# Attention's value products and score products of a gated cross-attention kernel, issued as 64x64 tiles of TensorE

## The chip, the cores and the metric

The kernel runs on one core of one Trainium2 chip. The metric is the device time of one execution in microseconds. The kernel before was timed three times: 958.02, 959.36 and 960.18 us, median 959.36 us. A profile is one further execution, recorded by the hardware profiler.

## The reference

Eight batches `b`, 1024 tokens each with `D` = 1024 features, attend to 64 memory rows of 512 features. All is fp32.

```python
memory_proj = einsum('bme,de->bmd', memory, W_mem)
scores = einsum('bnd,bmd->bnm', hidden, memory_proj) / sqrt(D)
attn = softmax(scores, axis=-1)
memory_context = einsum('bnm,bmd->bnd', attn, memory_proj)
gate_input = concatenate([hidden, memory_context], axis=-1)
gate = sigmoid(einsum('bnf,df->bnd', gate_input, W_gate) + b_gate)
fused = hidden + gate * memory_context
out = fused * rsqrt(mean(fused**2, axis=-1) + 1e-6) * norm_w
```

## The kernel before, in words

The tokens are cut into 16 groups `q` of 512 tokens, two groups to a batch. A group is four blocks of 128 tokens. In a setup stage the kernel projects the memory (`mp`, 64 rows by 1024) and multiplies the projected memory by the second half of the gate's weight. The two results stand one above the other in one tile `mg` of 128 partitions: rows 0 to 63 hold the projected memory, rows 64 to 127 its product with the gate weight and the bias. So `attn` times the upper half is `memory_context`, and `attn` times the lower half is that context's share of the gate's input.

The remaining large product is `x` times the first half of the gate's weight, 512 x 1024 by 1024 x 1024 for a group. It is computed with two nested levels of a Strassen-like scheme: seven outer products in the order `ORDER = (1, 6, 7, 5, 4, 2, 3)`, each of seven inner products of 128x128 by 128x256 (function `outer_product`). Each outer product accumulates in two PSUM banks, `af` and `ed`, for which there are two sets of names that alternate (`af0`, `ed0`, `af1`, `ed1`); two further inner products go to banks `b` (tile `kB`) and `c` (tile `kC`). The last two PSUM banks are a rotating pair with the tag `ctx`. VectorE (DVE) adds the inner sums `u2`, `u3`, `u4` and, with `fin_af` and `fin_ed`, adds a bank into the output rows (`gate` in the profile, `O` in the code). GpSimd (POOL) makes inner operand sums (`inner_s`) and part of the output sums (`pre`).

**Visits.** A visit (function `visit`) is the part of attention's value product that belongs to one row pair and one half of the 1024 columns: for each of the two blocks `r` it multiplies the transposed attention by `mg[0:64]` into a bank of its own (`pcs`, `pc` in the profile) and by `mg[64:128]` into `af` or `ed`, where it is added to the outer product's sum. Visits come in pairs, inside outer products 4 and 3, after the inner product `kC`: the visit of the outer product before last (5 or 2, whose banks `faf` and `fed` were kept), with its `pc` in banks `b` and `c`, and then the visit of the running outer product, with its `pc` in the `ctx` pair. There are 32 such pairs, two per group. ScalarE (ACT) then applies the sigmoid to a `gate` half, and DVE multiplies it by `pc` (function `gated`).

**Scores.** For each group, `scores` multiplies `mp` by the transposed tokens `A` over eight slices `k` of the features, one matmul for each of two row pairs `r`, all into bank `b`. ScalarE copies the bank to SBUF (`sT`); `transpose_scores` turns it by TensorE some slots later, and the softmax follows. The scores of group `q + 1` are issued inside outer product 3 of group `q`, directly after its two visits. Since bank `b` holds a `pc` there, ScalarE first copies that `pc` to SBUF (`pe`, L905), and the later multiplication reads the copy. The scores of group 0 stand between outer products 1 and 6 of group 0.

**Order.** The order within each engine is the order of the code: every instruction is pinned in program order. `plan` assigns side work to slots (`at`, 49 slots a group, one per inner product) or to named places inside an outer product (`mid` with a key; `beside.pop` runs it). In outer product 3 the named places come in this order: both visits, place `(q, 3, 0)`, the sums of the visit that was kept (`fin_af`, `fin_ed` of outer product 2, with their sigmoids), place `(q, 3)`, then the step to the next slot. Place `(q, 3, 0)` holds one DVE transpose of the next group's tokens; place `(q, 3)` holds the next group's scores, two large DVE sums (`outer_s` 1 and 2) and a normalisation.

Of the kernel before, what the change touches and what calls it, by code (L numbers as in the profile page):

```python
# [10 lines left out]
ALU = mybir.AluOpType  # L11
# [4 lines left out]
P = 128  # L16
# [4 lines left out]
def tile_gated_cross_attention_rmsnorm(  # L21
# [376 lines left out]

    def scores(q):

        pst = bank("b", [P, 2 * P], f"psT{q}")
        mpb = mps[q // QPB]
        for k in range(KD):
            for r in range(2):
                mm(
                    pst[r * M : (r + 1) * M, :],
                    mpb[:, k, :],
                    A[q, r, k // KH][:, k % KH, :],
                    k == 0,
                    k == KD - 1,  # L410
                )
        sTs[q] = t4k(small, [P, 2, P], "e", f"sT{q}")
        pin(nc.scalar.copy(sTs[q].rearrange("p t c -> p (t c)"), pst))

    def transpose_scores(q):
        sc = ps_ctx.tile([P, 4, M], F32, tag="ctx", name=f"sc{q}")
# [199 lines left out]
    def plan(q):  # L616
        t0 = SLOTS * q
        nxt = q + 1 < NQ
        for i, o in enumerate(ORDER):
            for part, t in ((0, 1), (1, 2)):  # L620
                if i + 1 < len(ORDER):
                    at(t0 + 7 * i + t, inner_s, q, ORDER[i + 1], part)
                elif nxt:
                    at(t0 + 7 * i + t, inner_s, q + 1, ORDER[0], part)
        if q == 0:
            at(t0 + 7, scores, q)
        at(t0 + (3 if q else 7), outer_s, q, 3)
        at(t0 + (11 if q else 22), outer_s, q, 4)
        at(t0 + 9, transpose_scores, q)
        at(t0 + 10, softmax_a, q)  # L630
        at(t0 + 13, softmax_b, q)
        at(t0 + 18, transpose_attn, q)
        at(t0 + 22, attn_difference, q)
        if not nxt:
            at(t0 + 5, load_last)
            return
        at(t0 + 2, load_xq, q + 1)
        for i, t, half in (
            (20, 0, 0), (21, 1, 0), (23, 2, 0), (25, 3, 0), (37, 2, 1), (38, 3, 1), (42, 0, 1)
        ):  # L640
            at(t0 + i, transpose_x, q + 1, t, half)
        mid((q, 3, 0), transpose_x, q + 1, 1, 1)
        mid((q, 3), scores, q + 1)
        mid((q, 3), outer_s, q + 1, 1)
        mid((q, 3), outer_s, q + 1, 2)
        if (q + 1) % QPB == 0:
            at(t0 + 10, load_mp, (q + 1) // QPB)
            at(t0 + 49, load_mg, (q + 1) // QPB)
        if q == 0:
            at(t0 + 8, add_bias, mgs[0][M:P, :])  # L650
            at(t0 + 20, add_bias, mgd[1, M:, :])
# [149 lines left out]
    EXT = {5: (1, 1, 2), 4: (1, 0, 2), 2: (0, 0, 0), 3: (0, 1, 4)}  # L801
    SECOND = {4: 5, 3: 2}
    NEG = {4: 6, 3: 7}
    sets = 0
    held = {}

    def visit(q, o, pcs, af, ed):

        row, h, g = EXT[o]
        at_, mg = attnTs[q], mgs[q // QPB]  # L810
        second = o in SECOND
        for r, k in ((0, af), (1, ed)):
            for n in range(2):
                cols = slice(h * H + n * C, h * H + (n + 1) * C)
                mm(
                    pcs[r][:, n * C : (n + 1) * C],
                    at_[0:M, 2 * row + r, :],
                    mg[0:M, cols],
                    n == 0,
                    True,  # L820
                )
                left = NEG[o] if second and r == 0 and n == 1 else g + r
                mm(k[:, n], at_[M:P, left, :], mg[M:P, cols], second and r == 1 and n == 0, True)

    def pre(q, o, u3, u4):

# [39 lines left out]
    def outer_product(q, o):  # L866

        nonlocal slot, sets
        l11, l12, l21, l22 = quarters(left(q, o))
        s1, s2, s3, s4 = (L2[q, o][:, i, :, :] for i in range(4))  # L870
        nxt = q + 1 < NQ
        af = bank(f"af{sets}", [P, 2, C], f"af{q}_{o}")
        ed = bank(f"ed{sets}", [P, 2, C], f"ed{q}_{o}")
        sets ^= 1
        second = o in SECOND

        def product(out, lhsT, s, start):
            nonlocal slot
            for k in range(2):
                mm(out, lhsT[:, k, :], w_op(o, s)[:, k, :], start and k == 0, k == 1)  # L880
            slot += 1

        ut = t4k(rot, [P, 4, C], "u", f"u{q}_{o}")
        p1, u2, u3, u4 = (ut[:, i, :] for i in range(4))
        step()
        product(af[:, 0], l11, R11, True)
        pin(nc.scalar.copy(p1, af[:, 0]))  # L887
        step()
        kb = bank("b", [P, C], f"kB{q}_{o}")
        product(kb, s2, T2, True)  # L890
        tt(nc.vector, u2, p1, kb, ALU.add)
        step()
        kc = bank("c", [P, C], f"kC{q}_{o}")
        product(kc, s3, R12, True)
        tt(nc.vector, u3, u2, kc, ALU.add)
        pre(q, o, u3, None)
        if second:
            f = SECOND[o]
            faf, fed, fu3, fu4 = held.pop((q, f))
            frow, fh, _ = EXT[f]  # L900
            fp = [bank(t, [P, H], f"pc{q}_{f}_{r}") for r, t in enumerate("bc")]
            visit(q, f, fp, faf, fed)
            if o == 3 and nxt:
                pe = t4k(small, [P, H], "pe", f"pe{q}")
                pin(nc.scalar.copy(pe, fp[0]))  # L905
                fp[0] = pe
            pcs = [ps_ctx.tile([P, H], F32, tag="ctx", name=f"pc{q}_{o}_{r}") for r in range(2)]
            visit(q, o, pcs, af, ed)
        for fn in beside.pop((q, o, 0), ()):
            fn()  # L910
        if second:
            one = slice(0, 1)
            fin_af(q, f, faf, fu4, one)
            gate(q, 2 * frow, fh, fp[0], 0)
            fin_ed(q, f, fed, fu3, one)
            gate(q, 2 * frow + 1, fh, fp[1], 1)
            rest = slice(1, 2)
            fin_af(q, f, faf, fu4, rest)
            fin_ed(q, f, fed, fu3, rest)
        for fn in beside.pop((q, o), ()):  # L920
            fn()
        step()
        product(ed[:, 0], l22, T4, not second)
        step()
        product(ed[:, 1], s1, T1, False)
        tt(nc.vector, u4, u2, ed[:, 1], ALU.add)
        pre(q, o, None, u4)
        first = o in SECOND.values()
        if first:
            held[q, o] = af, ed, u3, u4  # L930
        else:
            fin_ed(q, o, ed, u3)
        if second:
            row, h, _ = EXT[o]
            gate(q, 2 * row + 1, h, pcs[1], 2 if o == 3 and not nxt else 1)
        step()
        product(af[:, 1], s4, R22, False)
        step()
        product(af[:, 0], l12, R21, False)
        if not first:  # L940
            fin_af(q, o, af, u4)
        if second:
            if o == 4 and not nxt:
                at(slot + 1, gate, q, 2 * row, h, pcs[0], 1)
            else:
                gate(q, 2 * row, h, pcs[0], 1)
        if second and not nxt:
            c, d = 2 * row, 2 * row + 1
            if o == 3:
                sqrt_table()  # L950
            when = (3, 4, 4, None, 10, 11) if o == 4 else (0, 2, 2, 2, 3, 3)
            if o == 4:
                for h_ in range(2):
                    mid((q, 3, 0), last_weigh, c, h_)
            at(slot + when[0], last_root, d)
            at(slot + when[1], last_root, c)
            for w_, (t, h_) in zip(when[2:], ((d, 0), (d, 1), (c, 0), (c, 1))):
                if w_ is None:
                    mid((q, 3, 0), last_norm, t, h_)
                else:  # L960
                    at(slot + w_, last_norm, t, h_)
        elif second:

            c, d = 2 * row, 2 * row + 1
            for t in (d, c):
                at(slot + 5, residual, q, t)
            if row == 0:
                when = (17, 18, -1, None, 33, -2) if q + 2 < NQ else (17, 18, 20, 22, 24, 25)
            else:
                when = (17, 18, 22, 24, 29, 31)  # L970
            at(slot + when[0], square, q, c)
            at(slot + when[1], square, q, d)
            for w_, (t, h_) in zip(when[2:], ((c, 0), (c, 1), (d, 0), (d, 1))):
                if w_ is None:
                    mid((q + 1, 4), norm, q, t, h_)
                elif w_ < 0:
                    mid((q + 1, 4, 0) if w_ == -1 else (q + 1, 3), norm, q, t, h_)
                else:
                    at(slot + w_, norm, q, t, h_)
        del L2[q, o]  # L980
# [34 lines left out]
```

## Time and profile before

| | |
|---|---|
| median of three runs | 959.36 us |
| the profiled execution | 957.75 us |
| its span, first to last instruction | 956.0 us |
| granted TensorE clock | 0.997 |
| TensorE matmuls busy | 943.6 us, 99% of the span |
| VectorE busy | 811.4 us, 85% |
| GpSimd busy | 717.3 us, 75% |
| ScalarE busy | 371.0 us, 39% |

The page counts one fp32 matmul as two matmul records and two weight loads (PE and PEld), since it is run in two passes; 4984 records of each are 2492 matmuls. A form such as 64\*128 is the part of TensorE's array that an instruction uses, rows by columns: 128\*128 is the whole array, 64\*128 a row tile, 128\*64 a column tile. Matmuls overlap, so the distance between two starts, not the length of one record, is what a matmul costs in a stream.

### The profile page before, as it was taken

Reading aid. Unit: us, or ns where it says so; the run is one execution under the profiler, and the core shown is the slowest. Engines: PE = TensorE matmul, PEld = TensorE weight load, DVE = VectorE, ACT = ScalarE, POOL = GpSimd, SP = SyncE. Lnnn points to the kernel's source line nnn. Section 1 sums busy time; section 2 is a strip of 40 time slices with the busy share of each in tenths; the row PEclk is TensorE's granted clock in tenths of the full one; section 3 lists DMA queues with packets and bytes.
Section 4 is the critical chain, followed back from the end, with each engine's and each line's share of the span. In section 5 each row is a group of like instructions: output and inputs, shape, how many; then the busy total and the mean of one; then the engine's idle time right before and its main releaser. Section 6 shows DMA issues by size and latency. Waiting matters only on the chain.

```text
span 956.0 us, 14301 instructions
## 1 busy us (share of the span) xinstructions
PE 943.6 (99%) x4984; PEld 778.2 (81%) x4984; DVE 811.4 (85%) x1242; ACT 371.0 (39%) x797; POOL 717.3 (75%) x780
## 2 busy tenths in 40 slices
PE   9999999999999999999999999999999999999995
PEld 8546888888888888888888888888888888888884
DVE  6988888888888888888888888978888888878887
ACT  3001235262533535262433526252443526252456
POOL 4998877678676777787676867777686767877683
PEclk9999999999999999999999999999999999999998
DMA  9866674472919264481919265391918365390712
GB/s 381 270 152 152 113 126 107 123 164 52 202 45 196 91 138 117 110 177 43 211 45 186 84 147 125 93 194 32 222 46 173 92 143 133 85 203 26 217 67 89
DMA packets 70919, 128.33 MB, mean 134 GB/s; under 512 B 12352, under 2 KB 49216, under 8 KB 70592
## 3 DMA queue, kind: packets, MB, share of 16 engines
q1 hardware_dynamic: 61664, 93.86, 37.1%
q0 software_dynamic: 9184, 33.56, 19.2%
q8 instruction: 40, 0.66, 0.3%
q14 instruction: 31, 0.25, 0.1%
HBM read 87.56 MB, written 41.68 MB: 135 GB/s over the span
## 4 chain that ended last, share of the span: by engine, by line
PE 97%; DVE 1%; DMA 1%; ACT 0%; issue 0%; POOL 0%; SPq 0%; DVEq 0%
PE af L92 30%; PE ed L92 21%; PE pc L92 12%; PE kC L92 10%; PE kB L92 10%; PE psT L92 6%; PE pg L92 5%; PE pm L92 2%; DMA wm<-in_w_mem_t 1%; PE pa L451 0%; PE sc L420 0%; DVE gate L702 0%; DVE gate L776 0%; DVE u L95 0%; DVE gate L95 0%
## 5 line engine op out<-in xcount | busy, mean ns | idle before, releaser
L95 POOL TENSOR_TENSOR gate<-gate,u 128x512 f32<-128x512 f32 (+1 forms) x224 | 243.2, 1098 | 184.4 <-DVE u L95 148.5
L673 ACT ACTIVATE gate<-gate 128x512 f32<-128x512 f32 x128 | 79.9, 630 | 181.2 <-DVE gate L95 181.2
L352 DVE STREAM_TRANSPOSE a<-xq 128x512 f32<-128x512 f32 x128 | 141.0, 1105 | 3.3 <-POOL it L95 3.3
L95 POOL TENSOR_TENSOR l<-a 128x256 f32<-128x256 f32 x128 | 112.9, 882 | 18.7 <-PE af L92 17.4
L92 PE MATMUL pc<-mg,attnT 64*128 64x256 f32 x512 | 119.0, 383 | 0.3 <-DVE u L95 0.3
L702 DVE SCALAR_TENSOR_TENSOR gate<-gate,ss,nw_sb 128x512 f32<-128x512 f32 x120 | 115.6, 964 | 1.1
L92 PE MATMUL ed<-it,l 128*128 128x256 f32 x448 | 115.0, 379 | 0.0
L887 ACT COPY u<-af 128x256 f32<-128x256 f32 x112 | 40.7, 364 | 191.4 <-PE af L92 191.0
L92 PE MATMUL kB<-it,l 128*128 128x256 f32 x448 | 115.0, 379 | 0.0
L92 PEld LDWEIGHTS pc<-mg,attnT 64*128 64x128 f32 x512 | 93.2, 187 | 20.8 <-DVE u L95 11.0
L95 DVE TENSOR_TENSOR gate<-gate,pc 128x512 f32<-128x512 f32 x113 | 76.0, 683 | 31.7 <-ACT gate L673 31.7
L92 PE MATMUL af<-w,a 128*128 128x256 f32 x384 | 98.6, 379 | 0.0
L92 PEld LDWEIGHTS kB<-it,l 128*128 128x128 f32 x448 | 85.2, 190 | 11.5
L92 PEld LDWEIGHTS ed<-it,l 128*128 128x128 f32 x448 | 83.9, 190 | 10.7
L95 DVE TENSOR_TENSOR gate<-gate,ed 128x512 f32<-128x512 f32 x112 | 76.2, 680 | 18.0 <-POOL gate L95 17.7
L92 PEld LDWEIGHTS af<-w,a 128*128 128x128 f32 x384 | 73.0, 190 | 10.3 <-issue 0.5
L95 POOL TENSOR_TENSOR l<-s 128x256 f32<-128x256 f32 x96 | 78.4, 817 | 3.0 <-PE af L92 3.0
L95 DVE TENSOR_TENSOR gate<-gate,af 128x512 f32<-128x512 f32 (+1 forms) x128 | 76.3, 607 | 3.1 <-PE af L92 1.5
L92 PE MATMUL af<-mg,attnT 64*128 64x256 f32 x256 | 68.8, 389 | 0.0
L687 ACT ACTIVATE junk<-gate 128x1024 f32<-128x1024 f32 x60 | 63.5, 1058 | 10.8 <-DMA gate<-in_x 9.9
L92 PE MATMUL ed<-it,a 128*128 128x256 f32 x256 | 67.4, 386 | 0.0
L95 DVE TENSOR_TENSOR u<-u,kC 128x256 f32<-128x256 f32 x112 | 45.9, 410 | 23.8 <-PE kC L92 20.3
(140 smaller groups left out, 2030.9 us busy)
## 6 DMA issues: line engine op xcount, KB each, us to landing
xq<-in_x SPq DMA_DIRECT2D x64, 512.0 KB, 10.3
gate<-in_x POOLq DMA_DIRECT2D x60, 512.0 KB, 8.3
out<-gate SPq DMA_DIRECT2D x60, 512.0 KB, 3.5
w<-in_w_gate_t SPq DMA_DIRECT2D x8, 512.0 KB, 10.2
w<-in_w_gate_t SPq DMA_DIRECT2D x2, 2048.0 KB, 16.2
mg<-mgd SPq DMA_DIRECT2D x16, 256.0 KB, 6.1
wm<-in_w_mem_t SPq DMA_DIRECT2D x4, 512.0 KB, 6.3
mpd<-mpT SPq DMA_DIRECT2D x4, 512.0 KB, 7.1
```

The source lines that it names most:

```text
L92: pin(nc.tensor.matmul(o, lhsT, rhs, start=start, stop=stop, skip_group_check=True))
L95: pin(eng.tensor_tensor(o, a, b, op))
L352: nc.vector.transpose(A[key][:, :, r * P : (r + 1) * P], chunks(xq[q][:, 4 * t : 4 * t + 4, :], KD)[:, half * KH : (half + 1) * KH],)
L673: pin(nc.scalar.activation(g, g, AF.Sigmoid))
L687: nc.scalar.activation(junk, O[q, t], AF.Square, accum_out=ss[:, t % 2 : t % 2 + 1])
L702: nc.vector.scalar_tensor_tensor(g[:, cols], g[:, cols], rstd[:, t % 2 : t % 2 + 1], nw_sb[:, cols], ALU.mult, ALU.mult,)
L887: pin(nc.scalar.copy(p1, af[:, 0]))
```

## The change

Both `visit` and `scores` now issue every matmul on a 64x64 tile of the array. In a visit the 128 tokens of a block are split into two halves of 64 (`TOKENS`), each half a column tile, and the two chunks of 256 columns are joined into one matmul of 512, except for the one `af` product that needs two different left operands. In `scores` the 128 features of a slice are split into two halves of 64, which accumulate in two different banks: `b` and `c` for group 0, and the free set of `af` and `ed` for the others. ScalarE copies the first bank to `sT` as before, and the new `add_scores` adds the second bank to it on DVE, at slot 46 of the group (slot 8 for group 0). Since the scores no longer take bank `b`, the copy `pe` goes. The transpose at place `(q, 3, 0)` moves to a new place `(q, 3, 1)`, behind `fin_af` and `fin_ed`.

```diff
     def scores(q):
-        pst = bank("b", [P, 2 * P], f"psT{q}")
+        tags = (f"af{sets}", f"ed{sets}") if q else ("b", "c")
+        pst = [bank(t, [P, 2 * P], f"psT{q}_{t}") for t in tags]
         mpb = mps[q // QPB]
         for k in range(KD):
-            for r in range(2):
-                mm(
-                    pst[r * M : (r + 1) * M, :],
-                    mpb[:, k, :],
-                    A[q, r, k // KH][:, k % KH, :],
-                    k == 0,
-                    k == KD - 1,
-                )
-        sTs[q] = t4k(small, [P, 2, P], "e", f"sT{q}")
-        pin(nc.scalar.copy(sTs[q].rearrange("p t c -> p (t c)"), pst))
+            for g in range(2):
+                rows = slice(g * P // 2, (g + 1) * P // 2)
+                for r in range(2):
+                    mm(
+                        pst[g][r * M : (r + 1) * M, :],
+                        mpb[rows, k, :],
+                        A[q, r, k // KH][rows, k % KH, :],
+                        k == 0,
+                        k == KD - 1,
+                    )
+        sT = t4k(small, [P, 2, P], "e", f"sT{q}")
+        pin(nc.scalar.copy(sT.rearrange("p t c -> p (t c)"), pst[0]))
+        sTs[q] = sT, pst[1]
+
+    def add_scores(q):
+        sT, part = sTs[q]
+        flat = sT.rearrange("p t c -> p (t c)")
+        tt(nc.vector, flat, flat, part, ALU.add)
+        sTs[q] = sT
...
         if q == 0:
             at(t0 + 7, scores, q)
+            at(t0 + 8, add_scores, q)
...
-        mid((q, 3, 0), transpose_x, q + 1, 1, 1)
+        mid((q, 3, 1), transpose_x, q + 1, 1, 1)
         mid((q, 3), scores, q + 1)
+        at(t0 + 46, add_scores, q + 1)
...
+    TOKENS = slice(0, P // 2), slice(P // 2, P)
...
         for r, k in ((0, af), (1, ed)):
-            for n in range(2):
-                cols = slice(h * H + n * C, h * H + (n + 1) * C)
-                mm(
-                    pcs[r][:, n * C : (n + 1) * C],
-                    at_[0:M, 2 * row + r, :],
-                    mg[0:M, cols],
-                    n == 0,
-                    True,
-                )
-                left = NEG[o] if second and r == 0 and n == 1 else g + r
-                mm(k[:, n], at_[M:P, left, :], mg[M:P, cols], second and r == 1 and n == 0, True)
+            cols = slice(h * H, (h + 1) * H)
+            for t in TOKENS:
+                mm(pcs[r][t, :], at_[0:M, 2 * row + r, t], mg[0:M, cols], True, True)
+            if second and r == 0:
+                for n, left in ((0, g + r), (1, NEG[o])):
+                    part = mg[M:P, h * H + n * C : h * H + (n + 1) * C]
+                    for t in TOKENS:
+                        mm(k[t, n], at_[M:P, left, t], part, False, True)
+            else:
+                whole = k.rearrange("p n c -> p (n c)")
+                for t in TOKENS:
+                    mm(whole[t, :], at_[M:P, g + r, t], mg[M:P, cols], second, True)
...
             visit(q, f, fp, faf, fed)
-            if o == 3 and nxt:
-                pe = t4k(small, [P, H], "pe", f"pe{q}")
-                pin(nc.scalar.copy(pe, fp[0]))
-                fp[0] = pe
...
             fin_af(q, f, faf, fu4, rest)
             fin_ed(q, f, fed, fu3, rest)
+        for fn in beside.pop((q, o, 1), ()):
+            fn()
         for fn in beside.pop((q, o), ()):
             fn()
```

## The prediction

> **What bounds the kernel now.** I read the page first, shares and chain:
>
> ```profile
> span 956.0 us, 14301 instructions
> PE 943.6 (99%) x4984; PEld 778.2 (81%) x4984; DVE 811.4 (85%) x1242; ACT 371.0 (39%) x797; POOL 717.3 (75%) x780
> PE 97%; DVE 1%; DMA 1%; ACT 0%; issue 0%; POOL 0%; SPq 0%; DVEq 0%
> ```
>
> TensorE sets the end: 97% of the chain is PE, at a clock of 0.997. So the question is how much time PE's own stream takes, and whether any wait reaches it. Second, the timeline around outer product 3 of one group (start, us busy, engine; idle before in brackets):
>
> ```profile
> 181.34 1.10 DVE L352 STREAM_TRANSPOSE a<-xq 128x512 f32<-128x512 f32 x1
> ...
> 182.06 0.58 ACT L905 COPY pe<-pc 128x512 f32<-128x512 f32 x1 [2.36 <-PE af L92]
> ...
> 182.37 0.65 DVE L95 TENSOR_TENSOR gate<-gate,af 128x512 f32<-128x512 f32 x1
> ...
> 182.94 0.69 DVE L95 TENSOR_TENSOR gate<-gate,ed 128x512 f32<-128x512 f32 x1
> ...
> 184.02 0.38 PE L92 MATMUL pc<-mg,attnT 64*128 64x256 f32 x1
> ...
> 184.03 0.38 PE L92 MATMUL ed<-mg,attnT 64*128 64x256 f32 x1
> ...
> 184.24 0.38 PE L92 MATMUL pc<-mg,attnT 64*128 64x256 f32 x1
> 184.24 0.38 PE L92 MATMUL ed<-mg,attnT 64*128 64x256 f32 x1
> ...
> 184.55 3.67 PE L92 MATMUL psT<-a,mpb 128*64 128x256 f32 x32
> ...
> 188.15 1.13 PE L92 MATMUL ed<-it,s 128*128 128x256 f32 x4
> ...
> 190.19 0.42 DVE L95 TENSOR_TENSOR u<-u,ed 128x256 f32<-128x256 f32 x1 [0.96 <-PE ed L92]
> ```
>
> Two things are to be seen. The visits already run two matmuls at once, pc on the upper row tile and af or ed on the lower, a pair every 0.216 us; the scores run two at once as column tiles, 16 pairs in 184.55 to 188.15. And where the tile form changes there is a step: the last visit pair starts at 184.24, the scores could follow at 184.46 and do so at 184.55, 0.10 late. Third, the tile views of scores and visits (count, then min/median/max ns):
>
> ```profile
> L92 PEld LDWEIGHTS psT<-a,mpb x512: 132/137/138, 85.9 to 890.4; 128*64 128x64 f32 x171
> L92 PE MATMUL psT<-a,mpb x512: 378/379/431, 85.9 to 890.6; 128*64 128x256 f32 x171
> ```
> ```profile
> L92 PEld LDWEIGHTS pc<-mg,attnT x512: 182/187/188, 110.9 to 941.2; 64*128 64x128 f32 x171
> L92 PE MATMUL pc<-mg,attnT x512: 375/376/480, 110.9 to 941.4; 64*128 64x256 f32 x171
> ```
>
> The maxima are the first matmuls behind a change of form. Their weight load has nothing to hide behind: 480 less 376 is 0.10 us with 128 columns of weights, 431 less 379 is 0.05 with 64.
>
> **What the Trainium skill says.** "TensorEngine Tiling (Array Packing)", Tiling Modes: changing the tiling mode drains TensorE, changing the tile does not. The 0.10 us at each change of form agrees, and inside a form the pairs follow without a gap. "TensorE: Matmul & The Clock Gate", Part 3: row and column tiles compose, about 4 ns of issue for each further tile. This trace has only row pairs and column pairs, which start within 0.01 us of each other; four at once appear nowhere. Same page, LDWEIGHTS: the time goes with the columns, columns/1.2 ns, so 64 fewer should save 53; the trace has 187 against 137 ns.
>
> **The change part by part.**
>
> *Array time: nothing.* Before, a pair of visits is 16 matmuls of 256 columns, two passes each, two at once: 16 x 0.216 = 3.45 us. After, each of the four tiles takes half the tokens but 512 columns: per `r` two passes of 2 x 0.216, four `r` a pair of visits, 3.45 again. Scores before: 16 matmuls, two passes, two at once, 3.45. After: 32 matmuls, two passes, four at once, 3.45. Both forms filled the array already.
>
> *Visits to scores, 15 times.* Both are now 64x64, so the drain (0.10) and the open load of 64 columns (0.05) go: 15 x 0.15 = 2.2 us.
>
> *Into the visits, 32 times.* The change of form stays, with its 0.10; the open load has 64 columns in place of 128, if the four tiles load side by side as the pairs do now: 0.104 less 0.052, 32 x 0.052 = 1.7 us. Group 0's scores, and the way out of visits and scores to the full array, are as before.
>
> *Small terms.* Two more tiles start some 0.006 us apart each, about 0.013 a block, 32 blocks, +0.4. Against that, six of a tile's 16 matmul starts in a pair of visits go; at about 2.5 ns a start (an estimate from the skill's clock gate page, "Back-to-back issue gap"; this trace shows only the whole step of 0.216) that is 0.015 a pair, -0.5. They cancel.
>
> *Weight loads inside the stream: nothing.* In the visits they become fewer (36 for 64 records) and shorter; in the scores four loads of 0.137 share a 0.216 step, two of them in parallel today. Uncovered in the worst case, see the rivals.
>
> *`pe` removed:* 15 x 0.586 us of ACT, which idles 2.36 us before it. Nothing. The later multiplication reads bank `b` instead of SBUF; with both operands it takes 0.68 either way (pe and pc rows of the timeline).
>
> *Bank of the scores.* They waited for `pe` (done 182.64, scores at 184.55). Now they wait for `fin_af` and `fin_ed` of outer product 2. With the transpose out of the way `fin_af` can start when the first half of the kept visit is in, about 182.2; `fin_ed` needs the whole visit and starts at about 182.9 as now, ending at 183.63. The scores want the bank at 184.45: 0.8 us of cover in every group, since the trace repeats itself to 0.1 us. Behind a late `fin_ed` PE itself would stand still, and all after it.
>
> *The transpose* goes to about 183.6 to 184.7. The scores read its tile from slice `k` = 4, half way, at about 186.2: 1.5 us of cover. The normalisation and the two large sums behind it move 1.1 us back.
>
> *`add_scores`:* 16 x 0.42 us of DVE (the row u<-u,ed has the same 128x256 form) and a wait for the ACT copy at about 188.6. DVE reaches it at about 189.7 (two sums 1.1 later, then 0.68 for the first product), so it does not wait. Behind it stand the second product (bank `c`) and `u4`, `fin_ed` of outer product 3, then its sigmoid. `u4` has 0.96 us of idle time today and slips by roughly 0.5 net. Bank `b` is free at about 189.7 and wanted by the next group's kB at 192.57, bank `c` at about 190.8 and wanted at 193.44, `ed` for its first product at 194.30. DVE catches up in its 15% of idle time. POOL's and SP's queues carry the same instructions in the same order; the output store behind the normalisation leaves 1.1 us later. Nothing on the path; if that cover failed, each us late would cost up to 15 us.
>
> *Sum against the profiled execution:* 957.75 - 2.2 - 1.7 +- 0 = 953.85. The median of the runs stands 1.6 above the profiled execution, so 955.5 as a median.
>
> **Rivals.**
>
> *A, the likeliest, worked out above:* 955.5, own range 953 to 958.
>
> *B, slower: four tiles in the scores outrun PE's instruction supply.* Each fp32 matmul is two loads and two matmuls. A step of 0.216 us in the scores carries 4 of each, 27 ns an instruction; the densest stretch of this trace, visits or scores, carries 4 in a step, 54 ns. The skill (the clock gate page, "Wait — 56ns, not 53.3ns?") gives a floor of about 25 ns between matmul starts, which four matmuls in 0.216 clear with 54; whether loads count too it doesn't say. Against it: queued instructions are at hand when the scores begin. Price: at 35 ns a step takes 0.280, 16 steps x 16 groups x 0.064 = 16 us, so 972. It decides from 0.216 + 3.9/256 = 0.231 us a step, 29 ns an instruction.
>
> *C, slower by far: fp32 row and column tiling do not overlap,* four tiles run as two pairs. Array time doubles: 32 x 3.45 + 16 x 3.45 = 166 us, 1121. Nothing in the trace excludes it; the skill's measured composition speaks against it.
>
> *D, no change: the joint is smooth, but the four first loads go one behind the other.* An entry then costs 4 x 0.053 = 0.21 of open load in place of 0.104: 32 x 0.11 = +3.4, against -2.2: about 960.5. Or the drain remains at the joint because the scores' first matmul carries a DVE wait: then 1.7 less, 957.7.
>
> *E, slower: DVE late at the scores.* From 0.8 us of slip on, each 0.26 us more costs the whole gain (15 x 0.26 = 3.9). At 1.3 us, 963. The waits are worked out above with 0.8 left, so it is unlikely.
>
> **How the numbers follow.** A 0.75, B 0.09, C 0.04, D 0.09, E 0.03. A measurement of this kernel cannot tell less than about 0.2%, 1.9 us, from no change. Faster: A and a little of D, 0.77. Same: the rest of D and edges, 0.07. Slower: B, C, E, 0.16. The predicted time is A's. The range reaches from 953 (A, with noise of the runs) to 961.5 (D); B, C and most of E lie outside.
>
> **What would show it.** Right: visits and scores as 64\*64 forms, four starts within about 0.02 us; scores' matmuls starting 0.216 behind the last visit's; about 3.45 us a pair of visits and for the scores; the largest matmul of pc some 0.05 over its median instead of 0.10; PE's chain still 97%. Wrong: score steps longer than 0.216 (B), visit starts in two pairs 0.43 apart (C), an entry with loads in a row (D), scores' idle time put down to DVE (E).

## The result and the profile after

The changed kernel takes 956.12 us, median of eight runs (954.61 to 957.62), beside 958.74 us for the kernel before (eight runs, 958.02 to 960.18). The ratio is 0.9972, 95% interval 0.9962 to 0.9981: faster by 2.6 us, a little above what can be told from no change. The forecast was 3.9 us less. The measured time lies inside the range and only 0.6 us from the 955.5 named, but part of that closeness is luck: the 955.5 was counted from a median of three, 959.36, where eight runs give 958.74. The profiled execution took 956.04 us with a span of 954.0, against 957.75 and 956.0.

The page's shares and chain, as shown of the kernel before:

```profile
span 954.0 us, 15598 instructions
PE 940.2 (99%) x5624; PEld 730.9 (77%) x5624; DVE 807.5 (85%) x1258; ACT 362.9 (38%) x782; POOL 710.3 (74%) x780
PE 91%; DMA 4%; ACT 1%; DVE 1%; POOL 1%; issue 1%; SPq 0%; DVEq 0%
```

TensorE is still busy 99% of the span, but its share of the chain is 91 where it was 97, and DMA has 4% of the chain where it had 1%. First the timeline of TensorE at the joint of visits and scores, same group as before:

```profile
183.36 0.60 PE L92 MATMUL pc<-mg,attnT 64*64 64x512 f32 x2
183.38 0.60 PE L92 MATMUL ed<-mg,attnT 64*64 64x512 f32 x2
183.79 0.38 PE L92 MATMUL psT_af<-a,mpb 64*64 64x256 f32 x2
183.81 0.38 PE L92 MATMUL psT_ed<-a,mpb 64*64 64x256 f32 x2
184.00 0.38 PE L92 MATMUL psT_af<-a,mpb 64*64 64x256 f32 x2
184.02 0.38 PE L92 MATMUL psT_ed<-a,mpb 64*64 64x256 f32 x2
...
187.35 1.13 PE L92 MATMUL ed<-it,s 128*128 128x256 f32 x4
```

Each row is now two column tiles, two rows are the four tiles. Four start within 0.03 us. The steps are 0.43 for 512 columns and 0.216 for 256, and the scores begin 0.43 behind the last visit step: no step is left at the joint. (The prediction has 0.216 behind the last visit; as that visit's matmuls now have 512 columns, the stream asks 0.43.) The tile views (count, min/median/max ns):

```profile
L92 PE MATMUL psT_af<-a,mpb x480: 376/376/376, 130.0 to 888.7; 64*64 64x256 f32 x160
```
```profile
L92 PE MATMUL pc<-mg,attnT x512: 589/589/640, 110.6 to 939.2; 64*64 64x512 f32 x171
```

The scores' longest matmul is as long as their median (431 against 379 before): no open load. The visits' longest is 51 ns over the median, where it was 104. The four first loads go side by side. From the scores of group 1 to those of group 2 it is 53.79 us, where it was 54.05: 0.26 a group, 3.9 us in 15 groups, the forecast's sum. This distance, the group's period, is the surest measure here: in a trace it is the same to 0.01 us in nearly every group that waits for nothing, while the whole time also has the scatter of the setup stage in it.

So the gain is there in the stream, and part of it is given back elsewhere. The chain of the changed kernel between 300 and 325 us, in order of time, shows where:

```profile
301.06 0.59 POOL gate L689
301.65 14.38 DMA gate<-in_x
...
317.23 1.15 ACT junk L699 x2
...
318.40 1.28 ACT L704
...
320.00 0.36 ACT attnT L472
...
321.54 0.38 ACT u L901
...
322.06 2.83 PE af L92 x12
```

The DMA that adds `x` into finished rows (function `residual`) takes 14.4 us here; the median over all 60 is 8.4. ScalarE's `square` waits for it, and behind it on ScalarE's queue stand the second square, a table load, the root, four copies of the transposed attention and then the copy `p1` (u<-af), without which TensorE may not write the next product into `af`. In the timelines of ScalarE and TensorE the place is

```profile
316.05 1.06 ACT L699 ACTIVATE junk<-gate 128x1024 f32<-128x1024 f32 x1 [2.67 <-DMA gate<-in_x]
...
320.52 1.03 PE L92 MATMUL ed<-it,l 128*128 128x256 f32 x4
322.06 0.89 PE L92 MATMUL af<-t,l 128*128 128x256 f32 x3 [0.51 <-ACT u L901]
```

Four matmuls at 0.216 would bring the next start to 321.38; it comes at 322.06, 0.67 late. The same happens near 538 us (0.85) and 646 us (0.50), and 0.02 near 862: 2.05 us, and 0.3 more for weight loads that then lie open. The waits view has the two rows that tell it (us in total, times, longest). Of the kernel before it has only the first:

```profile
ACT junk L687 <- DMA gate<-in_x: 9.9, 7, 2.0
```

Of the changed kernel:

```profile
ACT junk L699 <- DMA gate<-in_x: 15.9, 8, 2.8
...
PE af L92 <- ACT u L901: 1.5, 3, 0.7
```

Seven of the eight waits are for rows of odd groups; in the stretch ahead of their DMA, SP loads a new batch's `mg` as well as tokens. The four that reached TensorE were waits of 2.67, 2.85, 2.50 and 2.02 us, and its starts came 0.67, 0.85, 0.50 and 0.02 late: what goes beyond 2.0 us arrives in full. This holds in every trace of this document in which the square has its old place: 24 late starts into `af`, each within 0.02 us of ScalarE's wait less 2.0, and none behind a shorter wait. Before, the longest wait was 1.97, and one start was 0.04 late: 2.0 us is what ScalarE's queue can hide, and the kernel before used all of it.

### The profile page after: what moved, and what is told of

It is laid out like the page before. It is cut to its first block, busy times and chain, and to the rows that moved or that the text cites. A ratio compares the mean times of both kernels' runs of the same rounds, so it can differ in the third digit from the quotient of the medians.

```text
span 954.0 us, 15598 instructions
## 1 busy us (share of the span) xinstructions
PE 940.2 (99%) x5624; PEld 730.9 (77%) x5624; DVE 807.5 (85%) x1258; ACT 362.9 (38%) x782; POOL 710.3 (74%) x780
## 4 chain that ended last, share of the span: by engine, by line
PE 91%; DMA 4%; ACT 1%; DVE 1%; POOL 1%; issue 1%; SPq 0%; DVEq 0%
PE af L92 29%; PE ed L92 19%; PE pc L92 10%; PE kC L92 9%; PE kB L92 9%; PE pg L92 5%; PE psT_af L92 5%; DMA gate<-in_x 3%; PE pm L92 2%; POOL l L95 1%; DMA wm<-in_w_mem_t 1%; PE psT_ed L92 0%; ACT attnT L472 0%; PE psT_b L92 0%; DVE gate L714 0%
## 5 line engine op out<-in xcount | busy, mean ns | idle before, releaser
L95 POOL TENSOR_TENSOR gate<-gate,u 128x512 f32<-128x512 f32 (+1 forms) x224 | 237.0, 1071 | 189.7 <-DVE u L95 153.8
L714 DVE SCALAR_TENSOR_TENSOR gate<-gate,ss,nw_sb 128x512 f32<-128x512 f32 x120 | 118.4, 987 | 1.1
L92 PE MATMUL pc<-mg,attnT 64*64 64x512 f32 x512 | 116.8, 595 | 0.3 <-DVE u L95 0.3
L95 DVE TENSOR_TENSOR gate<-gate,pc 128x512 f32<-128x512 f32 x128 | 86.2, 682 | 31.7 <-ACT gate L685 31.7
L92 PEld LDWEIGHTS ed<-it,l 128*128 128x128 f32 x448 | 83.9, 190 | 10.7
L92 PEld LDWEIGHTS af<-w,a 128*128 128x128 f32 x384 | 73.0, 190 | 10.3 <-issue 0.5
L92 PEld LDWEIGHTS pc<-mg,attnT 64*64 64x64 f32 x512 | 32.9, 132 | 50.2 <-issue 23.5
L92 PE MATMUL af<-mg,attnT 64*64 64x256 f32 (+1 forms) x384 | 67.4, 456 | 0.0
## 6 DMA issues: line engine op xcount, KB each, us to landing
xq<-in_x SPq DMA_DIRECT2D x64, 512.0 KB, 10.3
```

The source lines that it names most:

```text
L92: pin(nc.tensor.matmul(o, lhsT, rhs, start=start, stop=stop, skip_group_check=True))
L95: pin(eng.tensor_tensor(o, a, b, op))
L714: nc.vector.scalar_tensor_tensor(g[:, cols], g[:, cols], rstd[:, t % 2 : t % 2 + 1], nw_sb[:, cols], ALU.mult, ALU.mult,)
```

## The experiments

The theory for the missing part (T): the change made DVE run a normalisation later, with it its output store, and with the store the loads behind it on SP's queue. SP's timeline of the kernel before, for the group whose scores begin at 184.55, and of the changed kernel, where they begin at 183.79:

```profile
184.57 0.33 SPq L98 DMA_DIRECT2D out<-gate  x1
185.01 1.51 SPq L98 DMA_DIRECT2D mg<-mgd  x2
186.57 2.82 SPq L98 DMA_DIRECT2D xq<-in_x  x4
```
```profile
185.33 0.33 SPq L98 DMA_DIRECT2D out<-gate  x1
185.77 2.54 SPq L98 DMA_DIRECT2D mg<-mgd  x2
188.37 2.52 SPq L98 DMA_DIRECT2D xq<-in_x  x4
```

The store goes 1.5 us after the scores begin, where it went at once; the loads of `mg` follow as much later and those of the next tokens (`xq`) 2.6 us later, nearer to the accumulating DMAs issued 9.6 us after the scores. The rival (U): the late DMA has nothing to do with that order.

**Transpose put back.**

```diff
-        mid((q, 3, 1), transpose_x, q + 1, 1, 1)
+        mid((q, 3, 0), transpose_x, q + 1, 1, 1)
```

> The changed kernel with the one DVE transpose put back at its old place ahead of fin_af and fin_ed; tiles unchanged. Theory T: the normalisation behind the transpose ran later in the changed kernel (its output store was issued 1.55 us after the scores began, 0.1 in the kernel before), SP's loads of the next tokens stand behind that store, they meet the accumulating DMA of the tokens, ScalarE waits for that DMA (up to 2.85 us, 2.0 before) and three times the wait reached TensorE (0.7, 0.9, 0.5 us). With the transpose back the store should be issued near +0.7, ScalarE's longest wait for the DMA fall under 2.4 us, and the time be 1 to 2 us below the changed kernel's 956.1: ratio to the kernel before 0.9955 to 0.9963. Rival U: the late DMA is chance, or comes from groups that are 0.26 us shorter, and the order on DVE has nothing to do with it: ratio 0.997 as the changed kernel. Rival V: the transpose's old place makes fin_ed late and the scores wait for their bank: slower, a PE gap ahead of the scores in every group.

954.40 us (953.74 to 955.37), ratio 0.9957 (0.9944 to 0.9969), span 951.8. ScalarE's longest wait for the DMA is 2.2 and one start of TensorE is late, by 0.22. The scores did not wait for their bank, so V is out. This is as T expects, in this execution; the repetition below is less clear.

**Normalisation first.**

```diff
-                    mid((q + 1, 4, 0) if w_ == -1 else (q + 1, 3), norm, q, t, h_)
+                    mid((q + 1, 4, 0) if w_ == -1 else (q + 1, 3, 0), norm, q, t, h_)
```

> The changed kernel with the normalisation of the last quarter of a group moved from behind the transpose to ahead of fin_af and fin_ed. T: its store is issued some 2 us ahead of the scores, SP's loads 3.5 us earlier than in the changed kernel, no wait for the DMA reaches TensorE: the whole 3.9 us of the tile forms shows, ratio 0.9955 to 0.9962. U: 0.997. V: fin_ed some 0.3 us later, still ahead of the scores; if not, a gap ahead of the scores of up to 0.3 us in 15 groups, ratio 0.999.

954.52 us (953.56 to 954.88), ratio 0.9954 (0.9940 to 0.9967), longest wait for the DMA 1.8, no late start in `af`. The gain is as T has it, the size of the shift is not: the store went 1.8 us ahead of the scores, but the first load of tokens behind it only 1.3 to 1.6 us earlier than in the changed kernel, not 3.5, as SP's loads then wait for their buffers.

**Normalisation late.**

```diff
+        for fn in beside.pop((q, o, 2), ()):
+            fn()
         step()
...
-                    mid((q + 1, 4, 0) if w_ == -1 else (q + 1, 3), norm, q, t, h_)
+                    mid((q + 1, 4, 0) if w_ == -1 else (q + 1, 3, 2), norm, q, t, h_)
```

> The changed kernel with that normalisation moved the other way, behind the two large DVE sums, so that the store and the loads of the next tokens are issued some 3.5 us later still. T: ScalarE's waits for the accumulating DMA grow in most odd groups, PE waits of 1 to 3 us in five or more groups, 3 to 12 us slower than the changed kernel: ratio 1.000 to 1.010. U: 0.997, as the changed kernel.

959.79 us (956.86 to 962.14), ratio 1.0013 (1.0007 to 1.0020). The tiles are those of the changed kernel, yet the whole gain is gone:

```profile
ACT junk L699 <- DMA gate<-in_x: 27.6, 13, 3.2
...
PE af L92 <- ACT u L901: 2.7, 5, 1.1
```

Six starts of TensorE are late, by 0.24 to 1.25 us and 3.8 together, and even groups now wait too. The time is what T forecast, 3.7 us above the changed kernel; the late starts are shorter than its 1 to 3 us. So the order on DVE, and with it the time at which SP's store and loads go out, does bear on how late the accumulating DMA lands: U alone is out.

**The transpose's move alone, in the kernel before.**

```diff
-        mid((q, 3, 0), transpose_x, q + 1, 1, 1)
+        mid((q, 3, 1), transpose_x, q + 1, 1, 1)
...
+        for fn in beside.pop((q, o, 1), ()):
+            fn()
```

> The kernel before with only the transpose moved behind fin_af and fin_ed, as in the change; tiles, banks and copies as before. T: the store is issued near +1.3 us and PE waits for ScalarE appear that the kernel before does not have, 0.5 to 2.5 us in all: ratio 1.0005 to 1.0025. U: 1.000.

958.46 us against 958.46, ratio 1.0000 (0.9992 to 1.0008). T's number was wrong. The store is issued 1.3 us after the scores and ScalarE's waits for the DMA grow from 9.9 to 13.5 us, as T says, but the longest are 2.0 to 2.2, at the edge of what is hidden: 0.3 us of late starts and 0.3 of open loads. Whether the move costs more with the shorter groups of the new tiles is not shown by this run.

**Which tiles give the gain.** Four kernels stand on the one with the transpose put back (954.40 us). In the first the scores are column tiles again, in one bank:

```diff
-            for g in range(2):
-                rows = slice(g * P // 2, (g + 1) * P // 2)
-                for r in range(2):
-                    mm(pst[g][r * M : (r + 1) * M, :], mpb[rows, k, :], A[q, r, k // KH][rows, k % KH, :], ...)
+            for r in range(2):
+                mm(pst[r * M : (r + 1) * M, :], mpb[:, k, :], A[q, r, k // KH][:, k % KH, :], ...)
...
-        at(t0 + 46, add_scores, q + 1)
```

> The changed kernel with the transpose put back (the run with 954.4 us), and the scores as column tiles of 128x64 again, in one bank, without the addition; the visits stay 64x64. The theory of the prediction: the joint between visits and scores is a change of form again and costs 0.10 of drain and 0.05 of open weight load in 15 groups, so 2.2 us of the 3.9 are lost: ratio 0.9977 to 0.9985, and the first score matmul starts 0.10 later than the stream allows, with a maximum near 430 ns. Rival: the gain comes from the banks and the copy that went (pe), not from the tiles: ratio 0.9957.

956.75 us (956.06 to 958.03), ratio 0.9981 (0.9975 to 0.9988). The timeline of TensorE and the tile view have the step and the open load back:

```profile
184.24 0.60 PE L92 MATMUL pc<-mg,attnT 64*64 64x512 f32 x2
184.26 0.59 PE L92 MATMUL ed<-mg,attnT 64*64 64x512 f32 x2
184.79 0.44 PE L92 MATMUL psT<-a,mpb 128*64 128x256 f32 x2
```
```profile
L92 PE MATMUL psT<-a,mpb x512: 379/379/430, 86.4 to 889.9; 128*64 128x256 f32 x171
```

It is 0.55 from the last visit step to the scores, where the stream asks 0.43. The group's period is 53.94 us, 0.15 above the 53.79 of its base.

In the second the scores stay 64x64 and the visits are those of the kernel before:

```diff
-            for t in TOKENS:
-                mm(pcs[r][t, :], at_[0:M, 2 * row + r, t], mg[0:M, cols], True, True)
...
+            for n in range(2):
+                cols = slice(h * H + n * C, h * H + (n + 1) * C)
+                mm(pcs[r][:, n * C : (n + 1) * C], at_[0:M, 2 * row + r, :], mg[0:M, cols], n == 0, True)
...
```

> The same base (transpose put back), with the visits as the kernel before has them (64x128, 256 columns) and the scores 64x64. The theory of the prediction: both terms are lost, since the joint is a change of form and the visits open with 128 columns of weights: 3.9 us above the base, ratio 0.9995 to 1.0008. Rival (banks and the copy, not the tiles): 0.9957.

959.17 us (957.80 to 960.08), ratio 1.0007 (0.9998 to 1.0015): nothing is left. The tile view's longest pc matmul is 480 ns again, and the period is 54.06 us, where the kernel before has 54.05. The copy `pe` and its bank are gone in this kernel too, so they are worth nothing: the gain belongs to the tiles.

In the third all is 64x64, but the scores come one product later:

```diff
-        mid((q, 3), scores, q + 1)
-        at(t0 + 46, add_scores, q + 1)
+        at(t0 + 46, scores, q + 1)
+        at(t0 + 47, add_scores, q + 1)
```

> The same base with all tiles 64x64, but the scores one inner product later, behind the first product into ed, and their addition one slot later: the same instructions, one more change of form in and out of the scores. Theory: a way out of the visits (0.115 and 0.10 open load) and a way into the scores (0.09 and 0.05), 0.36 us in 15 groups, 5.4 us above the base: ratio 1.0008 to 1.002. Rival (the tile form itself is worth something, whatever its neighbours): 0.9957 to 0.997.

959.80 us (958.99 to 962.10), ratio 1.0015 (1.0008 to 1.0021), 5.4 us above its base (4.6 above the second run of that base, below), with a period of 54.15 us, 0.36 more. These are the instructions of the base, in an order that changes the form once more:

```profile
183.81 0.59 PE L92 MATMUL ed<-mg,attnT 64*64 64x512 f32 x2
184.34 1.13 PE L92 MATMUL ed<-it,s 128*128 128x256 f32 x4
185.40 0.43 PE L92 MATMUL psT_af<-a,mpb 64*64 64x256 f32 x2
```

Two matmuls of the full array take from 184.34 to 185.40, 1.06 in place of 4 x 0.216 = 0.86, since one pays the open load on the way out and the drain on the way in. So the 64x64 form in itself is worth nothing; what counts is the number of changes, and what the open load costs at each.

The fourth asks rival B: each score matmul cut in two.

```diff
-            for g in range(2):
...
-                    mm(pst[g][r * M : (r + 1) * M, :], mpb[rows, k, :], A[q, r, k // KH][rows, k % KH, :], ...)
+            for c in range(2):
+                for g in range(2):
...
+                        mm(pst[g][r * M : (r + 1) * M, c * P : (c + 1) * P], mpb[rows, k, :],
+                           A[q, r, k // KH][rows, k % KH, c * P : (c + 1) * P], ...)
```

> The same base with each score matmul cut into two of 128 columns: twice the loads and matmuls in the same array time, 13.5 ns an instruction in place of 27. Rival B of the prediction was that the supply of instructions limits four tiles. If supply has room: 32 steps of about 0.109 in place of 16 of 0.216, some 0.04 a group longer, 0.6 us above the base, ratio 0.996 to 0.9967. If it limits near 27 ns, the scores take 6.9 in place of 3.45 us: 55 us more, ratio 1.053; in between, the score step tells the ns an instruction.

956.48 us (955.27 to 958.75), ratio 0.9981 (0.9973 to 0.9989). TensorE's timeline:

```profile
184.94 0.28 PE L92 MATMUL psT_af<-a,mpb 64*64 64x128 f32 x2
184.95 0.28 PE L92 MATMUL psT_ed<-a,mpb 64*64 64x128 f32 x2
185.04 0.28 PE L92 MATMUL psT_af<-a,mpb 64*64 64x128 f32 x2
```

The steps are 0.109 us, eight instructions in each, 13.6 ns an instruction: the supply has room for twice what the change asks, and B is out. The period is 53.83 us, 0.04 above the base, which is the 0.6 us expected. The rest of the 2 us above the base is elsewhere; in this execution there are two late starts of the DMA kind (0.85 us, and 0.25 of open loads), a setup stage 1.1 us longer than in the base's profiled execution, and pauses inside the scores of two of the 16 groups (0.35 us near 349.6 and 0.11 near 835.8), for which the trace shows no wait. Whether the supply fell behind in these two is not known.

**Four on one chip.** The changed kernel once more:

> The changed kernel once more, beside the three others of this set on one chip. 956.1 +- 1: ratio 0.997.

956.06 us (954.67 to 957.48), ratio 0.9972 (0.9963 to 0.9981), the same as the first time.

The transpose put back, once more:

> The changed kernel with the transpose put back, once more. T (store and loads late on SP, DMA late, ScalarE waits, TensorE waits): 1 to 2 us under the changed kernel of this set, ratio 0.9957. If the two were only different draws of one distribution: both at about 0.9965.

955.25 us (953.94 to 956.83), ratio 0.9967 (0.9957 to 0.9978). By itself this can't be told from the changed kernel, and its profiled execution (956.08 us) has waits for the DMA of up to 3.0 us and two late starts, 1.8 us, although SP's store went out 0.3 us after the scores as in the first run of this kernel.

The traces do show the direction. The table has, counted from the start of the scores, when the first load of tokens is issued, and how long the second accumulating DMA, issued 10.3 us after that start, takes to land: means over the 7 groups in which SP loads `mg` too, and over the 6 in which it doesn't.

| kernel | with `mg`: load at, DMA takes | without: load at, DMA takes |
|---|---|---|
| before | 2.2, 13.1 us | 0.6, 10.1 us |
| before, transpose late | 3.4, 13.6 | 1.8, 10.8 |
| changed (two traces) | 3.6, 13.8 | 2.0, 11.4 |
| changed, transpose put back (two traces) | 2.5, 13.5 | 0.8, 10.7 |
| changed, normalisation first | 2.4, 13.2 | 0.4, 10.5 |
| changed, normalisation late | 5.7, 14.0 | 4.6, 13.6 |

In each pair that differs by one move on DVE, the DMA takes longer where the loads leave later. So the moved transpose does make the DMA later on average, by 0.3 us with `mg`. What TensorE loses hangs on the latest single ones, 14.5 and 14.7 us in the run above, and what makes these so late is not known. In time, both pairs lean the same way, by 1.7 and 0.8 us of the medians; how much of the changed kernel's loss the moved transpose causes stays open.

ScalarE's squares two slots later, everything else as in the changed kernel:

```diff
-                when = (17, 18, -1, None, 33, -2) if q + 2 < NQ else (17, 18, 20, 22, 24, 25)
+                when = (19, 20, -1, None, 33, -2) if q + 2 < NQ else (17, 18, 20, 22, 24, 25)
```

> The changed kernel with the transpose where the change has it, but ScalarE's two squares over the rows that the late DMA completes placed two slots later, behind the copies of the transposed attention. T: the DMA and SP stay as late as in the changed kernel, but the 1.5 us of copies no longer stand behind the wait, so it does not reach TensorE: ratio 0.9955 to 0.9963, as with the transpose put back, while ScalarE's wait ends at the same distance from the DMA's issue. If the cost came from DVE's order and not by way of ScalarE: 0.997.

954.04 us (954.01 to 954.75), ratio 0.9955 (0.9942 to 0.9967), the fastest median of all, and the five runs lie within 0.75 us where the changed kernel's lie within 3. The page:

```profile
span 952.0 us, 15598 instructions
...
PE 98%; DVE 1%; ACT 0%; issue 0%; POOL 0%; DVEq 0%
```

DMA is gone from the chain, and ScalarE's timeline in the group that lost 0.67 us above shows why:

```profile
315.06 1.51 ACT L472 COPY attnT<-pa 64x256 f32<-64x256 f32 x4 [1.30 <-PE pa L461]
316.47 1.06 ACT L699 ACTIVATE junk<-gate 128x1024 f32<-128x1024 f32 x1
```

The copies go first, and by then the DMA has landed; no square waits for it in any group. No start of TensorE into `af` is late. The span is 4.0 us below that of the kernel before: the forecast's 3.9. Two reservations: the latest DMA of this execution took 13.8 us, less than the 14.6 of the changed kernel's, and the move of the squares was not tried in the kernel before, where it may be worth something too (by medians this kernel is 4.8 us below it).

Both together:

> Transpose put back and squares two slots later. T: no TensorE wait for ScalarE left, the time of the stream alone, within 0.5 us of the run with the transpose put back: ratio 0.9952 to 0.996.

954.90 us (954.55 to 955.52), ratio 0.9962 (0.9949 to 0.9974), no late start into `af` either. It is no better than the squares alone, but its trace removes the first reservation: one DMA took 14.7 us here, as long as the longest of any run but the one with the late normalisation, and the waits view has no more than

```profile
ACT junk L699 <- DMA gate<-in_x: 0.2, 1, 0.2
```

At the old place of the squares, DMAs of 14.4 and 14.6 us made TensorE 0.67 and 0.85 us late. So the wait on ScalarE is the way by which the late DMA reaches TensorE.

## Why the prediction was right, and where its size was off

*Array time nothing; visits to scores 2.2 us; into the visits 1.7 us.* Shown, each by itself: with the joint's change of form back, 956.75 against 954.40 (2.3 us, or 1.5 against the second run of that base, 955.25); with the visits' loads back as well, 959.17 (2.4 more). The periods say it without the scatter: 53.79, then 53.94, then 54.06 us. One more change of form costs 0.36 us in each of 15 groups, 5.4 us, as worked out ahead of that run.

*Small terms cancel.* Nearly. The way out of 64x64 took 0.115 us in place of 0.097 for both former kinds; 32 times the difference is 0.6. The longer visit matmuls gave back about as much: from its first start to the next matmul of the full array, a pair of visits without scores behind it takes 3.599 us, where it was 3.654. Of these 0.055, the open load explains 0.052, and the way out went the other way by 0.018, so the stream inside became 0.02 shorter, 0.7 us in 32 pairs.

*Weight loads in the visits.* The prediction counts 36 for 64 and calls them fewer; a pair of visits had 32 and has 36. Nothing came of it, since the loads inside the stream stayed covered.

*Scores' bank, `add_scores`, `pe`.* Nothing, as costed: the scores begin without a gap in every group, and with `pe` gone but the tile gain taken away the kernel is no faster than before.

*"Nothing on the path" for the moved transpose and SP's store 1.1 us later.* This is the step that failed. The store was seen to leave later, but not what stands behind it on SP's queue, nor that the accumulating DMA, which lands later when those loads leave later, had a reader on ScalarE with its whole cover of 2.0 us already used. The kernel before showed the wait: 9.9 us in 7 waits, the longest 2.0. The term was set at 0; in the profiled execution it measured 2.05 us of late starts and 0.3 of open loads, and the sign that PE's chain would still be 97% failed with it. The sum 957.75 - 3.9 + 2.3 = 956.15 stands against 956.04 measured. With the squares moved the term is 0 and the forecast's sum is met: 954.0 in the profiled execution, where it said 953.85.

What sets the DMA's lateness in a given execution is only partly settled. On average it follows the loads, as the table shows, and the rows of odd groups suffer most; but single DMAs stray, and the transpose's share of the time is not clear of the scatter.

*Rivals.* B is out by the halved scores, C and D by the starts of four tiles, the 51 ns of open load and the joint without a drain, E by the absence of a gap at the scores. The two figures of issue that the prediction cites do not describe the starts on different tiles here: these lie 6 to 12 ns apart, neither 4 ns nor kept to a floor of 25.

## What to carry to other kernels

Where TensorE is the chain, count its changes of tile form and the columns of the first weights behind each: putting two stages that need different tiles into one common form, side by side, was worth 0.15 us a joint here, and the same tiles apart from each other cost 0.36. When the bound engine gets faster, look again for in-order queues whose cover was just enough: in the profiled executions ScalarE's wait for a DMA cost next to nothing in the kernel before and 2.3 us of a gain of 3.9 after. Here such a reader did best behind the short work that the bound engine needs from the same queue. And where a change is worth a few tenths of a per cent, compare the period of the loop in the traces: it separated 0.04 us a group, where the whole time scatters by up to 3 us between executions of the changed kernel.

## What the runs showed of the hardware

Four fp32 tiles of 64x64 run at the full rate of the array: starts 0.007 us apart on the two columns, about 0.02 for all four, steps of 0.216 us for 256 columns in two row and two column tiles together. With 128 columns the step is 0.109 us, so that TensorE is fed an instruction every 13.6 ns over the 3.5 us of a score stage, without a pause in 14 of 16 groups. The first loads of four tiles go in parallel, 51 ns open, just as for two.

A change of form cost 0.09 us on the way into a row, column or 64x64 form, 0.097 out of the first two and 0.115 out of 64x64, each beyond the step of the stream. The open load behind it cost 0.104 us with 128 columns of weights and 0.051 with 64.
